# Expert tokens scattered chunk by chunk, tile results summed in DRAM by accumulating scatters, and a last norm that reads whole blocks

## The chip, the cores and the metric

The kernel runs on one core of one Trainium2 chip. The metric is the device time of one execution, in microseconds: the median of five runs of the kernel before is 2193.05 us (2187.0 to 2196.98). TensorE is called PE here, VectorE DVE, ScalarE ACT, GpSimd POOL and SyncE SP. PE, DVE, ACT and POOL each work through their own instructions strictly in order; a DMA is issued from SP's or POOL's instruction stream and then runs beside the engines.

## The reference

A decoder of two layers on 16 sequences of 128 tokens, 512 wide, all in float32. Every sub-layer ends in `x = layernorm(x + sublayer(x))`. The change lies in the last sub-layer, a mixture of experts:

```
logits = x @ gate_weight.T;  scores = softmax(logits)            # 2048 tokens, 8 experts
topk_w, topk_idx = top_k(scores, 2)
y  = sum over the 2 chosen experts e:  w_e * (silu(x @ g_e) * (x @ u_e)) @ down_e    # 352 wide
y += (silu(x @ sg) * (x @ su)) @ shared_down                     # shared expert, 704 wide
x  = layernorm(x + y)
```

## The kernel before

The activations lie on the chip throughout as 16 blocks `x[b]` of 128 tokens by 512. The five sub-layers before the experts are left as they are. During the cross attention ahead of the experts (`attend(p5, ...)`), SP issues, from `prepare(0)`, the shared expert's weights, one DMA that fills the DRAM buffer `slots_x` with zeros (L851; 39 tiles of 128 rows, 9,984 KB), and after it the context `ct` of group 2, which PE transposes at L864. SP's DMAs share one queue and start in the order of issue.

The expert stage has four parts.

Routing and the shared expert's hidden layer. DVE works out each token's two experts, their weights `w12`, and its two slots (`slots`), so that all tokens of one expert stand in whole tiles of 128 rows: the 32 blocks' worth of token copies and the padding make `NT` = 39 tiles. Beside it PE works on 24 chunks of the shared expert (`hidden(n, g)`, four groups `g` of 512 tokens, two halves `n` of three chunks each). A chunk is the matmuls `pg` and `pu` (L999), ACT's silu `sg` (L1006) and DVE's product `act` (L1007). PSUM has three banks for `pg` and two for `pu`, so PE can be about two chunks ahead of DVE.

Token scatter. Once the slots are known, POOL issues 32 indirect DMAs in a row (L1047): block `b` is written to its first slots and to its second slots in `slots_x`.

The loop over 39 tiles. A tile `t` has its expert's weights `ew`, 128 rows of 17,408 bytes gathered by one indirect DMA from POOL (L1060), in three buffers; and its tokens `xs`, read from `slots_x` by SP (L1065). The step of the loop is, on PE: transpose tile `step` (L1070), transpose the activations of tile `step-2` (L1092), gate and up of tile `step-1` (`rg`, `ru`, L1080), down of tile `step-2` (`ry`, L1101), and a share of the shared expert's down projection (`po`, L137). The weights of tile `s+3` can be asked for when the down matmuls of tile `s` have freed their buffer; gate and up of tile `s+3` come after the down matmuls of tile `s+1`. DVE copies `ry` to SBUF (L1105) and SP writes it to `slots_y` (L1106). `EARLY` = 7 blocks of the shared down projection (six matmul pairs each) are dealt over the 39 steps.

The end. For each block: one of the nine remaining shared down projections on PE, added to `x[b]` by DVE (L1113); two indirect reads of the block's rows from `slots_y`, issued by POOL (L1158); for each DVE's `x[b] += weight * y` (L1162); statistics on DVE (L110, L112, L114), the power for the reciprocal root on POOL (L116), a shift on DVE (L1146), the normalised block on ACT (L1147) and its write from SP (L1148). Two PSUM banks hold the shared down projection, so PE can be two blocks ahead of L1113.

The order within an engine is the scheduler's, within these dependences.

Of the kernel before, what the change touches and what calls it, by code (L numbers as in the profile page):

```python
# [45 lines left out]
def decoder_kernel(ctx: ExitStack, tc: tile.TileContext, a: dict, out: bass.AP):  # L46
# [40 lines left out]
        nc.sync.dma_start(t, src)  # L87
        return t

    x = [xp.tile([P, D], F32, tag=f"x{b}", name=f"x{b}") for b in range(NB)]  # L90

    def load_x(b0, b1):
        for b in range(b0, b1):
# [705 lines left out]
    def load_shared():  # L799
# [6 lines left out]
        for n in range(2):  # L806
# [13 lines left out]
            for copy in range(2):  # L820
                r = copy * h + n * last
                nc.sync.dma_start(sw_dn[r : r + last, 5, :], dn[h : h + last, 2])
    slots_x = dram.tile([NT * P, D], F32, tag="slots_x", name="slots_x")
    slots_y = dram.tile([NT * P, D], F32, tag="slots_y", name="slots_y")

    with tc.tile_pool(name="p5", bufs=1) as p5:
        gate = moe.tile([P, KC, 32], F32, tag="gate", name="gate")
# [2 lines left out]
        irev = load_const("irev", [P, E], a["irev"], moe)  # L830
        before = moe.tile([P, P], F32, tag="before", name="before")
        nc.vector.tensor_tensor(before, maskT, ident, ALU.subtract)
        count = moe.tile([P, NB + NT + 1], mybir.dt.int32, tag="count", name="count")
        nc.gpsimd.iota(count[:, 0:NB], [[P, NB]], base=0, channel_multiplier=0)
        nc.gpsimd.iota(count[:, NB : NB + NT], [[1, NT]], base=0, channel_multiplier=0)
        nc.gpsimd.iota(count[:, NB + NT :], [[1, 1]], base=0, channel_multiplier=1)
        ramp = moe.tile([P, NB + NT + 1], F32, tag="ramp", name="ramp")
        nc.vector.tensor_copy(ramp, count)
        wq5, wo5 = wqo5[:, 0], wqo5[:, 1]
        psum.share(mm=2, sc=4, pt=2)  # L840
# [2 lines left out]
        def prepare(g):  # L843
            if g == NG:
                return []
            ct = load_context(g) if g else ct0
            if g == 0:
                load_shared()
                zero = p5.tile([P, D], F32, tag="zero", name="zero")
                nc.gpsimd.memset(zero, 0.0)  # L850
                nc.sync.dma_start(  # L851
                    slots_x.rearrange("(n p) d -> p n d", p=P), zero.unsqueeze(1).broadcast_to([P, NT, D])
                )
            ctT = p5.tile([P, TG], F32, tag="ctT", name="ctT", bufs=2)
            xT = p5.tile([P, KC, TG], F32, tag="xT", name="xT", bufs=2)
            qT = p5.tile([P, KC, TG], F32, tag="qT", name="qT", bufs=2)
            kT = p5.tile([P, KC, TG], F32, tag="kT", name="kT", bufs=2)
            vs = [p5.tile([P, D], F32, tag="v", name="v", bufs=2 * GB) for _ in range(GB)]
            groups[g] = qT, kT, vs

            def turn_context():
                pk = bank("mm", [P, GB, P], "pk")
                for i in range(GB):
                    nc.tensor.transpose(pk[:, i, :], ct[:, i, :], ident)  # L864
                nc.scalar.copy(ctT, pk.rearrange("p b l -> p (b l)"))

            tasks = [(0.64, turn_context)]
            tasks += [(0.64, lambda i=i: transpose_x(xT, g * GB + i, i * P)) for i in range(GB)]
            for c in range(KC):
                cols = slice(c * P, (c + 1) * P)  # L870
                chain(
                    tasks, "pk2", [(wkv5[:, cols], ctT)], lambda pk2, c=c: nc.vector.tensor_copy(kT[:, c, :], pk2)
                )
                chain(
                    tasks, "pq", [(wq5[:, k, cols], xT[:, k, :]) for k in range(KC)],
                    lambda pq, c=c: nc.scalar.mul(qT[:, c, :], pq, 1.0 / math.sqrt(HD)),
                )
            for i in range(GB):
                chain(
                    tasks, "pv", [(ctT[:, i * P : (i + 1) * P], wkv5[:, D : 2 * D])],  # L880
                    lambda pv, i=i: nc.scalar.copy(vs[i], pv),
                )
            return tasks
# [28 lines left out]
    with tc.tile_pool(name="p6", bufs=1, reuse_waits="tile") as p6:  # L912
        acts, halves = {}, {}
        w12 = []
        slots = []
        which = p6.tile([P, NT], mybir.dt.int32, tag="which", name="which")

        def half_rows(g):
# [14 lines left out]
        with tc.tile_pool(name="p6a", bufs=1, side="right", reuse_waits="tile") as p6a:  # L933
# [48 lines left out]
            both = gt("both")  # L982
            nc.vector.tensor_tensor(both, chosen[0], chosen[1], ALU.add)

            def hidden(n, g):


                if n == 0:
# [3 lines left out]
                for m_ in range(3 * n, 3 * n + 3):  # L992
                    whole = m_ < 5
                    pg = bank("sc", [P, TG], "pg")
                    pu = bank("pt", [P, TG], "pu") if whole else pg[FS % P :]
                    for dst, off in ((pg, 0), (pu, P))[: 2 if whole else 1]:
                        at = 2 * m_ * P + off
                        for k in range(KC):
                            nc.tensor.matmul(  # L999
                                dst, lhsT=sw_gu[:, k, at : at + P], rhs=xTs[g][:, k, :],  # L1000
                                start=(k == 0), stop=(k == KC - 1),
                            )
                    sg = p6.tile([P, TG], F32, tag="sg", name="sg", bufs=3)
                    rows = slice(0, P) if whole else slice(0, FS % P)
                    act = acts[g][:, m_, :] if whole else halves[g // 2][half_rows(g)]
                    nc.scalar.activation(sg[rows], pg[rows], AF.Silu)  # L1006
                    nc.vector.tensor_tensor(act, sg[rows], pu, ALU.mult)  # L1007

            hidden(0, 0)


# [26 lines left out]
            for n in range(2):  # L1038
# [2 lines left out]
                sl = p6.tile([P, NB], mybir.dt.int32, tag=f"slot{n}", name=f"slot{n}")  # L1041
                nc.vector.tensor_copy(sl, m)
                slots.append(sl)
            views = dram_disjoint_views(slots_x, 2 * NB)
            for b in range(NB):
                for n in range(2):
                    nc.gpsimd.indirect_dma_start(  # L1047
                        out=views[2 * b + n], out_offset=bass.IndirectOffsetOnAxis(ap=slots[n][:, b : b + 1], axis=0),
                        in_=x[b], in_offset=None,
                    )  # L1050


        table = a["l1f_w"].rearrange("n p f -> (n p) f")
        with tc.tile_pool(name="p6r", bufs=1, side="right", reuse_waits="tile") as p6r:

            class Tile:
                def __init__(self, t):
                    self.t = t
                    self.w = p6.tile([P, EW], F32, tag="ew", name=f"ew{t}", bufs=3)
                    nc.gpsimd.indirect_dma_start(  # L1060
                        out=self.w, out_offset=None, in_=table,
                        in_offset=bass.IndirectOffsetOnAxis(ap=which[:, t : t + 1], axis=0),
                    )
                    self.x = p6r.tile([P, D], F32, tag="xs", name="xs", bufs=3)
                    nc.sync.dma_start(self.x, slots_x[t * P : (t + 1) * P, :])  # L1065

                def turn(self):
                    tr = bank("mm", [P, KC, P], "tr")
                    for k in range(KC):
                        nc.tensor.transpose(tr[:, k, :], self.x[:, k * P : (k + 1) * P], ident)  # L1070
                    self.xT = p6r.tile([P, KC, P], F32, tag="xsT", name="xsT", bufs=2)
                    nc.scalar.copy(self.xT, tr)  # L1072

# [23 lines left out]
                def down(self):  # L1097
                    dn = down_w(self.w)
                    po = bank("av", [P, D], "ry")
                    for m_, mw in enumerate(ECH):  # L1100
                        nc.tensor.matmul(  # L1101
                            po, lhsT=self.actT[:mw, m_, :], rhs=dn[:mw, m_, :], start=(m_ == 0), stop=(m_ == 2)
                        )
                    y = p6.tile([P, D], F32, tag="y", name="ry", bufs=6)
                    nc.vector.tensor_copy(y, po)  # L1105
                    nc.sync.dma_start(slots_y[self.t * P : (self.t + 1) * P, :], y)  # L1106

            def shared_down(tasks, b):
                g, i = divmod(b, GB)
# [3 lines left out]
                    lambda po: nc.vector.tensor_tensor(x[b], x[b], po, ALU.add),  # L1113
                )

            ahead = {0: Tile(0)}
            for g in range(NG):
                for n in range(2):
                    if (n, g) != (0, 0):
                        hidden(n, g)  # L1120
                if g % 2:
                    ahead[len(ahead)] = Tile(len(ahead))
            EARLY = 7
            tasks = []
            for b in range(EARLY):
                shared_down(tasks, b)
# [1 line left out]
            for step in range(NT + 2):  # L1128
# [7 lines left out]
                    ahead.pop(step - 2).down()  # L1136
                if 3 <= step + 2 < NT:
                    ahead[step + 2] = Tile(step + 2)
                if step < NT:
                    share.deal()  # L1140


            def normalize(b, stats):
                mean, rstd = stats
                shift = small.tile([P, 1], F32, tag="shift", name="shift")
                nc.vector.tensor_scalar(shift, mean, rstd, -1.0, ALU.mult, ALU.mult)  # L1146
                nc.scalar.activation(x[b], x[b], AF.Identity, bias=shift, scale=rstd)  # L1147
                nc.sync.dma_start(out[b], x[b])  # L1148

            norms = []  # L1150
            for b in range(NB):
                if EARLY + b < NB:
                    tasks = []
                    shared_down(tasks, EARLY + b)
                    Share(tasks, 1).deal()
                for n in range(2):
                    y = p6.tile([P, D], F32, tag="y", name="yb", bufs=6)
                    nc.gpsimd.indirect_dma_start(  # L1158
                        out=y, out_offset=None, in_=slots_y,
                        in_offset=bass.IndirectOffsetOnAxis(ap=slots[n][:, b : b + 1], axis=0),  # L1160
                    )
                    nc.vector.scalar_tensor_tensor(x[b], y, w12[n][:, b : b + 1], x[b], ALU.mult, ALU.add)  # L1162
                norms.append((b, statistics(b, nc.vector)))
                if b:
                    normalize(*norms.pop(0))
            normalize(*norms.pop(0))
    psum.close()


# [122 lines left out]
```

## Time and profile before

| | |
|---|---|
| median of five runs | 2193.05 us (2187.0 to 2196.98) |
| the profiled execution | 2198.35 us, its span 2196.5 us |
| PE busy over the span | 2093.7 us, 95% |
| DVE, ACT, POOL busy | 880.8, 632.7, 502.1 us |
| 32 token scatters on POOL, L1047 | 31.1 us, 972 ns each |
| 39 weight gathers on POOL, L1060 | 36.9 us, 945 ns each |
| 32 reads of `slots_y` on POOL, L1158 | 32.3 us, 1009 ns each |
| software DMA queue (all indirect DMAs) | 103.68 MB, 12.8% of 16 engines over the span |
| from the last `ry` matmul's end to the span's end | 74.7 us (2121.8 to 2196.5) |

The span is the time from the first to the last profiled instruction of the program; the execution's time is 1.85 us longer. Busy time is summed over the span; a busy PE says which engine is full but not at which place an end is set, so the stages are read one by one. A wait "A <- B: us, times, longest" says how long A's engine stood still before A until B was done. "remote" stands where the profile cannot name what released it.

### The profile page before, as it was taken

How to read it: one execution, taken by the hardware profiler on the slowest of the kernel's cores; microseconds unless marked ns; L12 is line 12 of the kernel's file. 1: busy time of each engine (PE TensorE's matmuls, PEld its weight loads, DVE VectorE, ACT ScalarE, POOL GpSimd, SP SyncE). 2: the span in 40 equal slices, each digit the busy share in tenths (PEclk: the TensorE clock that was granted, in tenths of full speed). 3: DMA queues.
4: the chain of work that ended last, by engine and by line, in shares of the span. 5: the costliest groups of instructions: out<-in, count | busy, mean ns of one | idle time of the engine just before them, and what ended most of it. 6: DMA issues, size and time to landing. Idle time of an engine off the chain costs nothing.

```text
span 2196.5 us, 26727 instructions
## 1 busy us (share of the span) xinstructions
PE 2093.7 (95%) x10265; PEld 1178.2 (54%) x10265; DVE 880.8 (40%) x1700; ACT 632.7 (29%) x2174; POOL 502.1 (23%) x590
## 2 busy tenths in 40 slices
PE   7999997999999999999999999999898999999995
PEld 4555553445445458888555544555443455555542
DVE  4667644544333244222123324777430122122236
ACT  3555421333333222222211114566410111111102
POOL 4443320212111112323211101333232001001125
PEclk9999998999999999999999999999999999999998
DMA  5000253211000010001200026000033077787745
GB/s 220 1 33 33 102 149 99 70 38 33 6 10 6 1 40 14 1 1 50 99 1 1 1 56 223 1 1 1 1 118 131 2 266 298 292 299 296 290 173 177
DMA packets 73776, 199.63 MB, mean 91 GB/s; under 512 B 19760, under 2 KB 35504, under 8 KB 66992
## 3 DMA queue, kind: packets, MB, share of 16 engines
q1 hardware_dynamic: 62912, 94.24, 13.2%
q0 software_dynamic: 10736, 103.68, 12.8%
q8 instruction: 81, 1.33, 0.2%
q14 instruction: 47, 0.39, 0.1%
HBM read 163.82 MB, written 34.08 MB: 90 GB/s over the span
## 4 chain that ended last, share of the span: by engine, by line
PE 68%; issue 16%; DVE 6%; POOL 4%; DMA 3%; ACT 1%; another core or an unknown queue 1%; SPq 0%; POOLq 0%; ACTq 0%; DVEq 0%
PE po L572 10%; PE po L148 7%; PE pq L742 5%; PE pq L137 5%; PE pq L518 4%; PE pa L654 4%; PE pb L654 4%; PE po L681 4%; PE pg L999 3%; PE pu L999 3%; PE av L559 3%; PE pv L750 3%; DMA piece<-in_l0f_w_dram 2%; PE pt L203 2%; PE sc L535 2%
## 5 line engine op out<-in xcount | busy, mean ns | idle before, releaser
L198 POOL TENSOR_TENSOR p<-p,rs 128x512 f32<-128x512 f32 x192 | 199.3, 1039 | 579.3 <-DVE rs L197 567.1
L572 PE MATMUL po<-mT,cc 128*128 128x512 f32 x512 | 237.5, 608 | 0.0
L191 ACT ACTIVATE p<-t,nmx 128x128 f32<-128x128 f32 x512 | 198.6, 390 | 53.3 <-DVE nmx L186 27.4
L572 PEld LDWEIGHTS po<-mT,cc 128*128 128x128 f32 x512 | 92.9, 191 | 108.1 <-issue 104.4
L1060 POOL DMA_INDIRECT ew<-in_l1f_w_dram,which x39 | 36.9, 945 | 441.0 <-PE ry L1101 310.0
L191 ACT ACTIVATE p<-sc,nmx 128x128 f32<-128x128 f32 x256 | 90.0, 373 | 141.7 <-DVE nmx L186 131.4
L518 PE MATMUL pq<-xT,wqr 128*128 128x512 f32 x256 | 119.2, 609 | 0.9 <-ACT xT L128 0.7
L148 PE MATMUL po<-wo,oT 128*128 128x512 f32 x256 | 117.8, 604 | 1.0 <-ACT mT L292 0.6
L742 PE MATMUL pq<-xT,wq 128*128 128x512 f32 x256 | 110.9, 594 | 1.0 <-ACT xT L128 0.7
L1080 PE MATMUL rg<-ew,xsT 128*128 128x352 f32 x312 | 100.9, 466 | 6.3 <-DMA ew<-in_l1f_w_dram,which 6.2
L1101 PE MATMUL ry<-ew,ractT 128*128 128x512 f32 (+1 forms) x234 | 106.9, 592 | 0.0
L114 POOL TENSOR_SCALAR ve<-mv 128x1 f32<-128x1 f32 x80 | 17.9, 223 | 371.9 <-DVE mv L112 356.8
L1080 PE MATMUL ru<-ew,xsT 128*128 128x352 f32 x312 | 98.7, 459 | 0.0
L191 ACT ACTIVATION_READ_ACCUMULATOR p<-t,nmx 128x1 f32 x512 | 96.4, 188 | 0.0
L203 PEld LDWEIGHTS pt<-ident,p 128*128 128x128 f32 x512 | 60.5, 143 | 62.8 <-issue 50.8
L1087 DVE TENSOR_TENSOR ract<-rsg,ru 128x352 f32<-128x352 f32 x39 | 20.3, 521 | 175.1 <-issue 165.6
L203 PE MATMUL pt<-ident,p 128*128 128x128 f32 x512 | 79.4, 279 | 11.3 <-DVE pT L205 7.1
L121 DVE TENSOR_SCALAR x<-x,mv,rstd 128x512 f32<-128x512 f32 x80 | 53.7, 672 | 88.3 <-POOL rstd L116 88.3
L205 DVE COPY pT<-pt 128x512 f32<-128x512 f32 x128 | 86.7, 680 | 5.6 <-PE pt L203 5.3
L999 PE MATMUL pg<-xT,sw_gu 128*128 128x512 f32 x192 | 86.5, 593 | 0.0
L1072 ACT COPY xsT<-tr 128x512 f32<-128x512 f32 x39 | 22.8, 585 | 218.6 <-PE tr L1070 201.1
L137 PE MATMUL po<-sw_dn,act 128*128 128x512 f32 x160 | 78.3, 609 | 6.6 <-DVE ve L114 3.0
(210 smaller groups left out, 3676.4 us busy)
## 6 DMA issues: line engine op xcount, KB each, us to landing
piece<-in_l0f_w_dram SPq DMA_DIRECT2D x48, 352.0 KB, 3.3
raw<-in_l0x_raw_dram SPq DMA_DIRECT2D x8, 1728.0 KB, 6.9
slots_x<-zero SPq DMA_DIRECT2D x1, 9984.0 KB
xs<-slots_x SPq DMA_DIRECT2D x39, 256.0 KB, 9.0
slots_y<-ry SPq DMA_DIRECT2D x39, 256.0 KB, 2.2
x<-in_x_dram SPq DMA_DIRECT2D x16, 256.0 KB, 6.5
rep<-dkv SPq DMA_DIRECT2D x64, 64.0 KB, 1.9
out_dram<-x SPq DMA_DIRECT2D x16, 256.0 KB, 3.0
```

Of the source, the lines that this page charges most:

```text
L137: nc.tensor.matmul(got["p"], lhsT=lhsT, rhs=rhs, start=(n == 0), stop=(n == len(pairs) - 1))
L148: nc.tensor.matmul(po, lhsT=oT[:, c, :], rhs=wo[:, c, :], start=(c == 0), stop=(c == KC - 1))
L191: nc.scalar.activation(self.p[:, j, :], src[:, j, :], AF.Exp, bias=nmx[:, j : j + 1], accum_out=self.sm[:, j : j + 1])
L198: nc.gpsimd.tensor_tensor(self.p, self.p, spread(rs, P), ALU.mult)
L203: nc.tensor.transpose(pt[:, j, :], self.p[:, j, :], ident)
L518: nc.tensor.matmul(pq, lhsT=wqr[:, k, cols], rhs=xT[:, k, :], start=(k == 0), stop=(k == KC - 1))
L572: nc.tensor.matmul(self.po, lhsT=self.cc[:, 4 * par + j, :], rhs=mT[h], start=(par == 0 and j == 0), stop=(par == 1 and j == 3),)
L654: nc.tensor.matmul(dst, lhsT=wt[:, k, f * P : (f + 1) * P], rhs=xs[n][:, k, :], start=(k == 0 and n == 0), stop=(k == KC - 1 and n == 1),)
L742: nc.tensor.matmul(pq, lhsT=wq4[k // 2][:, k % 2, c * P : (c + 1) * P], rhs=xT[:, k, :], start=(k == 0), stop=(k == KC - 1))
L999: nc.tensor.matmul(dst, lhsT=sw_gu[:, k, at : at + P], rhs=xTs[g][:, k, :], start=(k == 0), stop=(k == KC - 1),)
L1080: nc.tensor.matmul(dst, lhsT=self.xT[:, k, :], rhs=gu[:, k, off : off + FE], start=(k == 0), stop=(k == KC - 1),)
L1101: nc.tensor.matmul(po, lhsT=self.actT[:mw, m_, :], rhs=dn[:mw, m_, :], start=(m_ == 0), stop=(m_ == 2))
```

## The change

There are four changes, all in the expert stage.

1. The blocks get four more columns (`xw`, 516 wide; `x[b]` is columns 2 to 513). In front and behind stand a token's weight and its token number, for the second and the first expert. `slots_x` rows are 516 wide. After the first three chunks, each chunk's end (`send`) lets POOL wait for the chunk's `act` (a copy of one column, `beat`) and then issue the two scatters of one block. The first weights are asked for after the third block's scatters.
2. A tile reads its rows' weight and token number with its tokens. `ry` is multiplied by the weight as it leaves PSUM, and POOL issues an indirect DMA that adds the tile's rows to the tokens' rows of a new DRAM buffer `sums` (padding rows go to rows past the tokens). `slots_y` and SP's writes to it are gone. `sums`, 55 blocks of 128 rows by 512, is zeroed by a second DMA right after that of `slots_x`. Since an addition reads and writes its rows, each of these scatters waits for the one before it to have landed.
3. At the end, SP reads `sums` in 16 plain blocks; POOL adds each to `x[b]`; the 32 indirect reads and DVE's 32 multiply-adds are gone. Epsilon, power and shift are made for two blocks at a time.
4. `EARLY` is 8, and the eight blocks left are dealt over seven parts of the end.

```diff
-    x = [xp.tile([P, D], F32, tag=f"x{b}", name=f"x{b}") for b in range(NB)]
+    xw = [xp.tile([P, D + 4], F32, tag=f"x{b}", name=f"x{b}") for b in range(NB)]
+    x = [t[:, 2 : D + 2] for t in xw]
...
-    slots_y = dram.tile([NT * P, D], F32, tag="slots_y", name="slots_y")
+    slots_x = dram.tile([NT * P, D + 4], F32, tag="slots_x", name="slots_x")
+    sums = dram.tile([(NB + NT) * P, D], F32, tag="sums", name="sums")
...
+                for t, rows, width in ((slots_x, NT, D + 4), (sums, NB + NT, D)):
+                    nc.sync.dma_start(
+                        t.rearrange("(n p) d -> p n d", p=P), zero[:, 0:width].unsqueeze(1).broadcast_to([P, rows, width])
+                    )
...
+                    if then is not None:
+                        then(act)
...
             for b in range(NB):
                 for n in range(2):
-                    nc.gpsimd.indirect_dma_start(
-                        out=views[2 * b + n], out_offset=bass.IndirectOffsetOnAxis(ap=slots[n][:, b : b + 1], axis=0),
-                        in_=x[b], in_offset=None,
-                    )
+                    at = D + 2 - n * (D + 2)
+                    nc.vector.tensor_copy(xw[b][:, at : at + 2], infos[n][:, b, :])
+        def send(act):
+            if unsent:
+                b = unsent.pop(0)
+                tc.keep_in_program_order(nc.gpsimd.tensor_copy(beat[0 : act.shape[0]], act[:, 0:1]))
+                for n in range(2):
+                    at = 2 - 2 * n
+                    tc.keep_in_program_order(nc.gpsimd.indirect_dma_start(
+                        out=views[2 * b + n], element_offset=at,
+                        out_offset=bass.IndirectOffsetOnAxis(ap=slots[n][:, b : b + 1], axis=0),
+                        in_=xw[b][:, at : at + D + 2], in_offset=None,
+                    ))
...
+                    info = p6r.tile([P, 2], F32, tag="tell", name="tell", bufs=6)
+                    nc.vector.tensor_tensor(info, self.x[:, 0:2], self.x[:, D + 2 : D + 4], ALU.add)
+                    self.weight = info[:, 0:1]
+                    self.place = p6r.tile([P, 1], mybir.dt.int32, tag="place", name="place", bufs=6)
+                    own = NC + NB + self.t
+                    nc.vector.tensor_tensor(self.place, info[:, 1:2], ramp[:, own : own + 1], ALU.add)
...
-                    nc.vector.tensor_copy(y, po)
-                    nc.sync.dma_start(slots_y[self.t * P : (self.t + 1) * P, :], y)
+                    nc.vector.tensor_scalar(y, po, self.weight, None, ALU.mult)
+                    nc.gpsimd.indirect_dma_start(
+                        out=sums, out_offset=bass.IndirectOffsetOnAxis(ap=self.place, axis=0),
+                        in_=y, in_offset=None, compute_op=ALU.add,
+                    )
...
-            EARLY = 7
+            EARLY = 8
...
+            share = Share(tasks, NB // 2 - 1)
+            for b in range(NB):
+                if b % 8 == 0:
+                    y = p6.tile([P, 8, D], F32, tag="ew", name=f"sum{b}", bufs=3)
+                nc.sync.dma_start(y[:, b % 8], sums[b * P : (b + 1) * P, :])
+                ys.append(y[:, b % 8])
...
+            for b in range(0, NB, 2):
+                if share.part < share.parts:
+                    share.deal()
+                mv = small.tile([P, 2, 2], F32, tag="mv2", name="mv2")
+                for i in range(2):
+                    nc.gpsimd.tensor_tensor(x[b + i], x[b + i], ys[b + i], ALU.add)
+                    st = small.tile([P, 6], F32, tag="st", name="st")
+                    nc.vector.bn_stats(st, x[b + i])
+                    nc.vector.bn_aggr(mv[:, i], st)
+                normalize(b, mv)
```

## The prediction

> **What bounds the kernel now.** PE is 95% busy, so the questions are where the other 5% lies in the stages that change, and what each edit puts in its place. I read the stages' windows first, then the waits, then the timeline at the two places where PE stands still.
>
> The windows (per engine: busy us and instructions; then granted clock, DMA share, GB/s):
>
> ```profile
> core 0: us, PE busy (x) PEld busy (x) DVE busy (x) ACT busy (x) POOL busy (x), PEclk, DMA share, GB/s
> ...
> 1650.00:1672.00 22.00, 15.99 (x37) 6.82 (x36) 1.34 (x2) 1.68 (x3) 12.27 (x13) 0.89 0.52 201
> 1672.00:1755.00 83.00, 83.00 (x193) 36.67 (x192) 8.96 (x13) 7.15 (x12) 0.98 (x1) 0.99 0.07 27
> ...
> 1790.00:2080.00 290.00, 284.45 (x964) 163.26 (x963) 60.20 (x129) 32.50 (x62) 28.28 (x31) 1.00 0.79 294
> ...
> 2122.00:2197.00 75.00, 49.77 (x104) 18.53 (x102) 43.17 (x106) 13.01 (x16) 42.12 (x48) 0.88 0.57 172
> ```
>
> Three places: a hole of 6 us in the chunks while the scatters run; the tile loop, where PE is full (284.45 of 290) and the DMA engines nearly so (0.79); and the end, 75 us of which PE works 50. The waits:
>
> ```profile
> POOL ew L1060 <- PE ry L1101: 310.0, 36, 14.0
> ...
> ACT sg L1006 <- remote: 24.7, 2, 12.8
> DVE act L1007 <- remote: 21.6, 1, 21.6
> ...
> PE rg L1080 <- DMA ew<-in_l1f_w_dram,which: 6.2, 12, 1.4
> PE pu L999 <- DVE act L1007: 6.0, 1, 6.0
> ```
>
> During the 32 scatters (1625.3 to 1665.9) ACT and DVE stood up to 21.6 us before `sg` and `act`, though PE's matmuls for them were done, until 1670.2, when the scatters had landed; PE filled its PSUM banks and then stood 6.0 us. In the loop POOL is idle until PE's down matmuls free a buffer, and PE meets late weights in 12 steps: PE and the weights' latency are level.
>
> The timeline of the end (start, duration; in brackets the idle before):
>
> ```profile
> 2119.03 2.74 PE L1101 MATMUL ry<-ew,ractT 128*128 128x512 f32 x6
> ...
> 2164.57 6.25 PE L137 MATMUL po<-sw_dn,act 128*128 128x512 f32 x10 [3.03 <-DVE ve L114]
> ...
> 2177.22 1.12 PE L137 MATMUL po<-sw_dn,half 64*128 64x512 f32 x2
> ...
> 2187.52 0.81 ACT L1147 ACTIVATE x<-x,shift,rstd 128x512 f32<-128x512 f32 x1 [3.43 <-DVE shift L1146]
> ```
>
> From the last `ry` (2121.8) PE needs 56.5 us to its last matmul (2178.3), then 10.0 us pass to ACT's last end (2188.3) and 8.2 to the span's end. A block's down projection takes 5.54 us (2125.33 to 2130.87 from one block's start to the next), and 1.7 us of the nine (a row of four matmuls at 2117.31) lie ahead of that `ry`: 9 x 5.54 - 1.7 = 48.2. So PE lost 8.3 us to DVE's queue and to the slower matmuls after a stall (ten in 6.25 us instead of 4.56).
>
> **The change, part by part.** The sum is made against the profiled execution, 2198.35 us, which is 5.3 us above the median.
>
> *Scatters in pairs.* Two scatters per chunk of 6.87 us instead of 32 in 41 us. POOL is otherwise idle there; the last pair goes after the 19th chunk, five chunks (34 us) ahead of the loop. PE waits for nothing on POOL. The cause of the late releases is not named in the profile; they began after about 18 scatters had followed one another, and nothing of the kind stands elsewhere. I take it that they go: 6.0 us of standing, and 1.8 us since the eight matmuls after it took 5.23 us instead of 3.43. Gain 7.8 (between 0, if they come anyway, and 7.8). DVE's 32 copies of two columns (147 ns like L114) and four small pieces, about 5.5 us, follow the slots at 1625.6 and end at 1631.2, 0.5 us past the next `act` (1630.7): PE, two chunks ahead, covers that. The weights of tile 0 are asked for some 25 us later, and are first needed at 1756.8.
>
> *A second zero fill.* The first fills 4992 rows from 1331 to about 1358 at 352 GB/s, DMA share 0.98. 7040 rows more take 27 x 7040/4992 = 38 us, to 1396, and the context of group 2 is behind them in SP's queue: it lands at about 1400. PE transposes it at 1404.3 and all behind it on PE would wait. Margin 4 us; rows of 2,064 bytes could use it up. I take 1 us (0 to 8, if the first fill's rows run 25% slower and cost 7 us, and the rest 5).
>
> *The loop: DVE and SP.* The weighted copy is read from PSUM as the copy was (692 ns); two small DVE pieces per tile, 0.3 us, lie in DVE's idle time (60 of 290 us busy). SP loses 39 writes. Nothing on the path.
>
> *The loop: the adding scatters.* POOL issues one per step (about 1 us) and has 9.4 us (tile 3's weights are issued at 1770.88, tile 38's at 2099.64: 9.39 a step). Order on POOL: weights of `s+3`, adding scatter of `s`, weights of `s+4`. The scatter is queued behind 2.2 MB of weights, whose last rows end 10.1 us after their issue, so it lands some 13 us after it, and the next scatter waits for that: about 4 us into the next step. That wait holds up the following weights only if it grows by 4 us more.
> What counts is the DMA engines' time. By the packet records a weight row takes 648 ns, eight rows on each engine 5.2 us; next to it 0.67 for `xs` (8 x 84 ns) and 0.67 for the write of `y`, which goes. A plain scatter of 256 KB takes 4 packets of 159 ns on each engine, 0.64 us. No row shows an addition. Its floor is that plain price; its ceiling is eight rows one after another at the latency of a first packet after a pause (1.0 to 1.8 us, mostly 1.2), 9.6 us. Packets in this queue follow each other without such gaps (648 ns on end), so I take it near the floor: one more row moved per row written, 1.3 us. Between the weights' last rows (10.1) and the next weights' first (9.4 + 2.2) the queue has 1.5 us free. So most of it is hidden; I let a quarter of the added 0.6 us delay the weights. The price of 1 us of delay: weights of `s+3` land, gate and up 4.74, down 2.57, and two steps have passed, so half a microsecond a step, 18 us over 36 steps. 0.17 x 18 = 3 us.
> The Trainium skill (Collectives: The Full Stack, "Why ReduceScatter is half of AllGather") has it that an addition in the DMA path costs no adder time but a second source read on the same ring, so that the rate halves. By it the scatter takes twice the plain 0.64 us and the 3 us stand; by the plain row alone the ring gains nothing and loses nothing and the 3 us fall away. No run here shows an addition yet.
>
> *One block more in the loop.* 12 matmuls, 5.2 us at the `po` pace of 0.86 a pair. Where PE waits for weights (12 of 36 steps) they cost nothing: 4 (3 to 5.2).
>
> *The end.* Before the first sum can be read, the scatters of tiles 36 to 38 must land one after another: `ry` 0.9, issue 1.0, landing 2 to 3, then SP's read, about 8 us after the last `ry`; the first `slots_y` read came after 9.1 (2130.92). From there POOL needs 16 adds at 1.27 us (L729, the same shape) and 8 powers at 0.57: 25 us, done 33 us after the last `ry`. PE needs 8 x 5.54 - 1.7 = 42.6. In DVE's order the sum of the third block left stands behind the statistics of block 9, which POOL reaches about 21 us after the last `ry`; PE wants that bank at 22. So PE stands little: 1 us (0 to 8.3, its loss now). Behind PE's last matmul: DVE's add 0.7, POOL's 1.3, statistics 0.9, epsilon 0.15, power 0.55, shift 0.2, two blocks on ACT 1.6, hand-overs 0.5: 5.9 us instead of 10.0, since no indirect read's multiply-adds are left. The end: 42.6 + 1 + 5.9 + 8.2 = 57.7 instead of 74.7, gain 17.0.
>
> *Sum:* 2198.35 - 7.8 + 1 + 3 + 4 - 17.0 = 2181.6; by the median, 5.3 less, 2176.
>
> **The rivals.**
> *The addition is slow* (slower). The one mechanism: an adding scatter holds its queue for x us an engine, and the next weights wait. Over the 1.5 us that are free each microsecond costs 18. For: the DMA share of 0.79, PE already meeting late weights, and that each row must be read before it can be written. Against: POOL's and the queue's free gap. The other terms gain 19.8, so it decides from x = 2.6, four plain scatters. At x = 4: 45 us instead of 3, 2218. At the ceiling of 9.6 a step has 5.2 + 0.7 + 9.6 = 15.5 instead of 9.4: +220, about 2393.
> *The late releases stay.* If scatters as such, not their density, hold up ACT and DVE, 7.8 us stay: 2184. For: the cause is not named. Against: the waits begin only after 18 of them.
> *The end does not shrink.* If POOL's adds, DVE's order or the serial scatters hold PE's two banks as the reads do now, its 8.3 us of loss stay, and a late context takes its 8: 2176 + 7 + 7 = 2190.
>
> **How the numbers follow.** Five runs spread by 0.45%; I count under 0.3%, 6.6 us, as no change: 2186.5 to 2199.6. My forecast 0.54 (2166 to 2186, from no loop cost and no stall at all to 10 us of them); late releases 0.10, most of it still faster; the end as it is 0.09; slow addition 0.27, nearly all past 2199.6. Faster 0.61, same 0.12, slower 0.27. The range runs from 2166 to 2225, where a slow addition of x = 4 is inside and only its far part is out.
>
> **What would show it.** Right: no "remote" wait in the chunks and PE's windows full there; no wait of PE for `ct` near 1404; a step of 9.3 to 9.5 us with PE's waits for `ew` under 10 us; about 58 us from the last `ry` to the span's end, PE without holes in it. Wrong: steps of 10 us and more with PE waiting for `ew`, scatters landing over 13 us after their issue, POOL standing before weights on an earlier scatter; or the second fill in the way of `ct`.

## The result, and the profile after

The changed kernel took 2201.18 us (median of 33 runs, 2196.16 to 2207.95), the kernel before 2195.74 us (59 runs). The ratio is 1.0032, with a 95% interval of 1.0023 to 1.0040: a third of a per cent slower, where 0.8% faster was forecast. The profiled execution took 2201.42 us (span 2199.6). The same windows of it (busy us and instructions per engine; then granted clock, DMA share, GB/s):

```profile
core 0: us, PE busy (x) PEld busy (x) DVE busy (x) ACT busy (x) POOL busy (x), PEclk, DMA share, GB/s
...
1360.00:1404.00 44.00, 42.90 (x286) 23.87 (x284) 33.20 (x65) 31.82 (x136) 15.68 (x17) 1.00 0.98 357
...
1650.00:1672.00 22.00, 22.00 (x53) 9.80 (x52) 2.07 (x3) 1.79 (x3) 7.33 (x10) 1.00 0.19 72
...
1790.00:2080.00 290.00, 273.50 (x922) 154.95 (x921) 60.42 (x185) 30.46 (x59) 75.01 (x59) 1.00 0.84 276
...
2122.00:2200.00 78.00, 62.17 (x142) 25.44 (x140) 28.60 (x66) 12.51 (x17) 27.32 (x27) 0.92 0.42 130
```

The hole among the chunks is closed: 22.00 of 22 us, where it was 15.99. The second fill fills the DMA engines (0.98) and PE doesn't mind. But the loop, where PE was busy for 284.45 of 290 us, now has 273.50. Its waits, from 1755 to 2139 us (engine, line, waited for: us in total, times, longest us):

```profile
engine line waited for: us in total, times, longest us
DVE tell L1108 <- DMA xs<-slots_x: 263.1, 34, 9.0
POOL ew L1093 <- PE ry L1143: 223.2, 36, 20.1
...
PEld rt L1134 <- DVE ract L1129: 26.2, 23, 4.8
PE rt L1134 <- DVE ract L1129: 20.8, 21, 4.5
```

PE no longer waits for weights (it was 6.2 us in 12 steps). It waits for `ract`, a DVE instruction that it never met late before. And DVE, idle for most of the loop, has a wait that didn't exist: `tell`, on the token load `xs`. One step in the timeline shows how the two belong together (first PE, then DVE: start, duration, in brackets the idle time before and what ended it):

```profile
1953.85 2.53 PE L1122 MATMUL ru<-ew,xsT 128*128 128x352 f32 x8
...
1959.65 0.60 PE L1106 MATMUL tr<-ident,xs 128*128 128x128 f32 x4
1961.68 0.55 PE L1134 MATMUL rt<-ident,ract 128*128 128x128 f32 x3 [1.43 <-DVE ract L1129]
```

```profile
1961.00 0.16 DVE L1108 TENSOR_TENSOR tell<-xs 128x2 f32<-128x2 f32 x1 [8.70 <-DMA xs<-slots_x]
1961.11 0.52 DVE L1129 TENSOR_TENSOR ract<-rsg,ru 128x352 f32<-128x352 f32 x1
```

PE had finished `ru` of tile 20 at 1956.38, so `ract` could have run then. It ran at 1961.11, since `tell` stood ahead of it in DVE's queue. That `tell` belongs to tile 24: its load was issued at 1951.19, its last row ended 9.2 us later, and PE turns tile 24 only at 1979.18. The scheduler had put DVE's reading of the tile right behind the tile's load, four tiles ahead, in front of work that PE needed at once.

By stages, worked out from the starts and ends of PE's instructions in the traces (us; the forecast is the sum of its steps; the fifth column is an experiment below):

| stage | before | forecast | after | `tell` held |
|---|---|---|---|---|
| to the first routing matmul `plT` | 1583.7 | 1584.7 | 1584.8 | 1576.9 |
| chunks, to the first `rg` | 173.1 | 165.3 | 165.3 | 165.3 |
| loop, first `rg` to last `ry` | 365.0 | 372.0 | 388.9 | 363.6 |
| last `ry` to PE's last matmul | 56.6 | 43.6 | 50.2 | 51.3 |
| PE's last to the span's end | 18.2 | 14.1 | 10.4 | 10.4 |

The first row is the same code but for the fill, and lies between 1576 and 1585 in all the profiles of this case; the long ones have the lower granted clock there (0.98 at 1584.8 us here, 0.99 at 1576.2 in the last experiment). The other rows repeat within 2 us where the code is the same. So the forecast failed in the loop, by 17 us, and at the end by 3.

### The profile page after: what moved, and what is told of

It reads as the page before. It is cut to its first block, busy times and chain, and to the rows that moved or that the text cites. A ratio compares the mean times of both kernels' runs of the same rounds, so it can differ in the third digit from the quotient of the medians.

```text
span 2199.6 us, 26823 instructions
## 1 busy us (share of the span) xinstructions
PE 2095.7 (95%) x10265; PEld 1180.1 (54%) x10265; DVE 868.0 (39%) x1766; ACT 631.9 (29%) x2174; POOL 544.6 (25%) x624
## 4 chain that ended last, share of the span: by engine, by line
PE 78%; DMA 9%; DVE 6%; issue 3%; POOL 2%; ACT 1%; ACTq 0%; SPq 0%; POOLq 0%; DVEq 0%
PE po L574 10%; PE po L150 7%; DMA xs<-slots_x 6%; PE pq L744 5%; PE pq L139 5%; PE pq L520 4%; PE pg L1008 4%; PE pa L656 4%; PE pb L656 4%; PE po L683 4%; PE pu L1008 3%; PE ry L1143 3%; PE av L561 3%; PE rg L1122 3%; PE pv L752 2%
## 5 line engine op out<-in xcount | busy, mean ns | idle before, releaser
L1108 DVE TENSOR_TENSOR tell<-xs 128x2 f32<-128x2 f32 x39 | 6.3, 161 | 272.9 <-DMA xs<-slots_x 272.9
L205 PEld LDWEIGHTS pt<-ident,p 128*128 128x128 f32 x512 | 60.2, 142 | 62.2 <-issue 53.3
L1114 ACT COPY xsT<-tr 128x512 f32<-128x512 f32 x39 | 22.8, 585 | 226.6 <-PE tr L1106 197.4
L667 POOL TENSOR_TENSOR hl<-ht,hh 128x512 fp32r<-128x512 f32 x44 | 58.1, 1320 | 116.7 <-ACT hh L665 116.7
```

What stands on the lines that cost most here:

```text
L205: nc.tensor.transpose(pt[:, j, :], self.p[:, j, :], ident)
```

## The experiments

All of them stand against runs of the kernel before on the same chip.

**`tell` held in its place.** One line of the changed kernel:

```diff
-                    nc.vector.tensor_tensor(info, self.x[:, 0:2], self.x[:, D + 2 : D + 4], ALU.add)
+                    tc.keep_in_program_order(
+                        nc.vector.tensor_tensor(info, self.x[:, 0:2], self.x[:, D + 2 : D + 4], ALU.add)
+                    )
```

> The changed kernel with one thing altered: `tell`, the small DVE addition that reads a fetched tile's side columns, is held in DVE's order where the program writes it (behind the weighted copy `ry` of the step before) instead of where the scheduler put it (ahead of `ract`, some 21 us before PE turns the same tile). Theory A, DVE's queue: in the changed kernel's loop DVE stood 263 us in 34 waits for the token loads `xs`, with `ract` queued behind, and PE lost 20.8 us in 21 waits for `ract`, 4.5 of it at the loop's start. If that is the cause, the waits of DVE for `xs` go, PE's waits for `ract` go, PE meets late weights again as before (6 us), the step falls from 9.88 to 9.4-9.5 us, first `rg` to last `ry` falls from 388.9 to 369-373 us, and the time to 2181-2185 us. Theory B, the transfers: if the adding scatters take so much of the DMA engines that loads land late, the wait only moves to the weights or to `xs` on PE; the step stays at 9.8-9.9 and the time at 2198-2204 us.

Measured: 2170.0 us, ratio 0.9877 (0.9852 to 0.9903). In the loop PE waited for one thing only (the same columns as the waits above):

```profile
PE rg L1124 <- DMA ew<-in_l1f_w_dram,which: 2.5, 2, 1.5
```

And DVE in one step (the columns of the timeline):

```profile
1922.32 0.52 DVE L1131 TENSOR_TENSOR ract<-rsg,ru 128x352 f32<-128x352 f32 x1 [4.58 <-PE ru L1124]
...
1924.83 0.75 DVE L1149 TENSOR_SCALAR ry<-ry,tell 128x512 f32<-128x512 f32 x1 [1.99 <-PE ry L1145]
...
1925.50 0.15 DVE L1109 TENSOR_TENSOR tell<-xs 128x2 f32<-128x2 f32 x1
```

`ract` now waits for PE, not for a load, and `tell` waits for nothing: its tile has long landed. The loop fell from 388.9 to 363.6 us, below the kernel before, though it holds a block more. The time fell further than I had expected (2181 to 2185), because I had put back the late weights of the kernel before (6 us), of which 2.5 came, and the 3 us of the forecast for the addition, of which the loop shows next to nothing (below). By their ratios the two changed kernels lie 34 us apart, by the stages behind the first routing matmul 24; the rest shows in none of these stages and stays open.

**The one instruction alone, in the kernel before.**

```diff
                         nc.tensor.transpose(tr[:, k, :], self.x[:, k * P : (k + 1) * P], ident)
+                    info = p6r.tile([P, 2], F32, tag="tell", name="tell", bufs=6)
+                    nc.vector.tensor_tensor(info, self.x[:, 0:2], self.x[:, D - 2 : D], ALU.add)
```

> The kernel before with one instruction added per tile: DVE adds two columns of the fetched tile `xs` to two others (128 x 2) into a small tile that nobody reads. Everything else, the scatters in one block, plain writes, the indirect reads at the end, stays as before; here too the scheduler has put the small addition ahead of `ract`. Theory A: this one instruction of 0.16 us brings most of the loop's loss: DVE waits for `xs` in some 35 steps, PE for `ract` in 20 or more, the step rises from 9.39 to 9.7-9.9 us and the time by 10 to 20 us, to 2206-2216. Theory B: 39 x 0.16 us beside idle time of DVE: 2194-2198 us.

Measured: 2215.47 us, ratio 1.0087 (1.0063 to 1.0110); the step 9.71 us, the loop 381.9 instead of 365.0. Its waits, with the same columns as above:

```profile
DVE tell L1072 <- DMA xs<-slots_x: 263.9, 35, 9.1
...
PE rt L1094 <- DVE ract L1089: 20.8, 22, 3.7
```

An addition of 128 x 2 elements that nobody reads costs 17 us of loop, with no adding scatter in the kernel. Its 39 executions are busy for 6 us.

**Plain scatters for adding ones, twice.** First in the changed kernel as it is:

```diff
-                        in_=y, in_offset=None, compute_op=ALU.add,
+                        in_=y, in_offset=None,
```

> The changed kernel with plain scatters in place of the adding ones (same rows, same queue, same waits); it leaves out the addition of a token's two results, so the sums hold only one of them. Theory A, DVE's queue: nothing of what `ract` waits for has changed; PE still loses about 20 us to it: 2196-2203 us. Theory B, the addition's own transfers: the step falls to 9.4-9.5 us and the time to 2181-2186 us. By my forecast's own term the addition is worth 3 us at most, if its cost shows in the loop at all.

Measured: 2199.63 us, ratio 1.0023 (1.0006 to 1.0040). The loop took 389.8 us, against 388.9 with the addition: the addition is not what lengthened it. Then the same edit with `tell` held:

> The kernel with `tell` held in place, and plain scatters in place of the adding ones; it leaves out the addition of a token's two results. This is the price of the addition where DVE's queue no longer hides it. An adding scatter's rows took 8 x 184 ns on each engine, plain ones 4 x 160 ns: 0.83 us a step less. With `tell` held PE has 2.5 us of waits for weights left. If the addition's time lies in the queue's gaps: 2168-2171 us, the same as with it. If it delays the weights by the quarter that I took: up to 2.5 us less, 2167-2168 us. The slow addition of my rival (45 us and more) would show as a far larger gain, which the 2.5 us that are left to wait for rule out.

Measured: 2168.23 us, ratio 0.9858 (0.9837 to 0.9879); the loop 362.9 against 363.6 and, in a second profile of the kernel with `tell` held, 363.0. The addition costs the loop at most 0.7 us (362.6 to 363.6 us with it in four profiles, 362.9 without), too little to tell from nothing. Its transfers do take longer, 184 ns on average for each of eight rows on an engine against 160 ns for a pair of rows: 1.47 against 0.64 us, and POOL is busy for 1.59 instead of 0.99 us.

What the addition costs lies at the end. DVE, POOL and ACT work through the same instructions in the same order there, with additions and with plain writes, but with plain writes PE needs 43.8 us from the last `ry` to its last matmul, where the two profiles with additions have 51.3 and 49.8 (without `tell` held 43.7 against 50.2). The last tile's scatter waits until the one before it has landed. As an addition it was issued 2.8 to 3.3 us after the last `ry` and its last row ended 4.3 to 4.4 us later; as a plain write, 1.1 and 2.4. So POOL's first additions of the read sums begin 10.3 to 10.8 us after the last `ry`, and 6.6 to 6.7 with plain writes (POOL in the changed kernel, whose last `ry` ends at 2139.0; then POOL and PE in this one, 2109.7):

```profile
2149.26 4.42 POOL L1222 TENSOR_TENSOR x<-x,sum 128x512 f32<-128x512 f32 x4 [6.00 <-DMA sum<-sums]
```

```profile
2116.36 4.23 POOL L1224 TENSOR_TENSOR x<-x,sum 128x512 f32<-128x512 f32 x4 [4.68 <-DMA sum<-sums]
...
2131.22 4.56 PE L139 MATMUL po<-sw_dn,act 128*128 128x512 f32 x10 [1.31 <-DVE x L1160]
```

PE's longest stop in the end is 1.31 us here and 4.35 with additions. Behind PE's last matmul 3.4 us of the gain are lost again (13.8 instead of 10.4; see the last section).

**The scatter issued twice, into one table and into two.** Both with `tell` held.

```diff
                         in_=y, in_offset=None, compute_op=ALU.add,
                     )
+                    nc.gpsimd.indirect_dma_start(
+                        out=sums, out_offset=bass.IndirectOffsetOnAxis(ap=self.place, axis=0),
+                        in_=y, in_offset=None, compute_op=ALU.add,
+                    )
```

> The kernel with `tell` held in place, and each adding scatter issued twice; the sums hold each result twice. It asks from where the rival of the slow addition decides. A second scatter adds 8 x 184 ns = 1.47 us to every engine's step (5.2 for weights, 0.67 for `xs`, 1.47 for the first: 8.8 of 9.33 us) and 1.6 us to POOL's. By my forecast's rule (1.5 us free, each further us costs 18) 2.94 us of scatter cost 26 us: about 2196 us. If the free time is larger than I took: 2170-2180. If POOL stands until the first scatter has landed (some 8 us) before it may issue the second, and the next weights are queued behind that: the step grows by several us, 2230 us and more.

Measured: 2376.99 us, ratio 1.0816 (1.0796 to 1.0836), a step of 14.94 us. My rule gave 2196; the last of the three cases came, and stronger. POOL and PE in the timeline, one step:

```profile
1997.74 4.05 PE L1124 MATMUL rg<-ew,xsT 128*128 128x352 f32 x8 [3.49 <-DMA ew<-in_l1f_w_dram,which]
...
1999.68 1.55 POOL L1154 DMA_INDIRECT sums<-ry,place  x1 [8.35 <-DMA sums<-ry,place]
...
2001.54 1.00 POOL L1093 DMA_INDIRECT ew<-in_l1f_w_dram,which  x1 [0.31 <-issue]
```

The second scatter waits 8.35 us for the first to land, and the next weights are queued behind it on POOL. To tell that wait from the transfers, the second scatter then went to a table of its own (`out=spare`, the same size):

> The kernel with `tell` held in place; behind each adding scatter a second one adds the same rows to a second table of the same size that nobody reads (nor fills first). The same DMA work and the same 1.6 us of POOL as with each scatter issued twice into one table (2377 us, step 14.94), but the second no longer waits for the first to land. If the engines' and POOL's time made the 206 us: about 2377 again. If it was the wait (POOL stood 294 us in 39 waits for the first scatter, with the next weights queued behind): by my forecast's rule of 18 us per us over the free 1.5 us, 2.94 us of scatters cost 26 us, 2190-2205; with more room in the queue than I took, 2170-2185.

Measured: 2181.14 us, ratio 0.9935 (0.9915 to 0.9954). The loop took 371.8 us, 8 to 9 more than with one scatter, and PE met late weights again (8.8 us in 9 waits). So 2.94 us of adding transfers a step cost 8 us, not the 26 of my rule, and nearly all of the 207 us was the wait with what followed from it. With both scatters in one table the loop grew by 195 us (558.2): 117 are standing, and most of the rest are matmuls behind a stop, at a lower granted clock (0.88 over the loop, 1.00 with one scatter); the eight of `rg` above took 4.05 us instead of 2.53. These scatters are dear on POOL by what they wait for, not by what they move.

**The scatters spread, in the kernel before.** The token scatters two per chunk, the tiles fetched after them; nothing else of the change:

```diff
+        def send(act):
+            if unsent:
+                b = unsent.pop(0)
+                tc.keep_in_program_order(nc.gpsimd.tensor_copy(beat[0 : act.shape[0]], act[:, 0:1]))
+                for n in range(2):
+                    tc.keep_in_program_order(nc.gpsimd.indirect_dma_start(
...
-                        hidden(n, g)
-                if g % 2:
+                        hidden(n, g, send)
+                if g != 2:
```

> The kernel before with its 32 token scatters issued two per chunk, after each chunk's activations, instead of one after another; the tiles are fetched after the last of them; the rest as before. My forecast gave this part a gain of 7.8 us: no wait of ACT or DVE that ends on a late release, PE's 22 us window from 1650 full, 2188 us (2186-2190). Its rival, that the late releases come with scatters as such: 2195-2197 us and the same waits of 10 to 20 us elsewhere in the chunks.

Measured: 2188.55 us, ratio 0.9969 (0.9955 to 0.9983). The chunks took 165.3 us from the first routing matmul to the first `rg`, as in the changed kernel, instead of 173.1. Then the same kernel with all 32 scatters behind the first chunk:

```diff
             if unsent:
-                b = unsent.pop(0)
                 tc.keep_in_program_order(nc.gpsimd.tensor_copy(beat[0 : act.shape[0]], act[:, 0:1]))
+            while unsent:
+                b = unsent.pop(0)
                 for n in range(2):
```

> The kernel before with everything that the spread version of it has (weights of tile 0 asked for later, tiles fetched after the scatters, POOL's small copy that ties the first scatter to a chunk), but all 32 scatters behind the first chunk, one after another. If the density of the scatters makes ACT and DVE see PE's releases late: waits of 10 to 20 us of ACT `sg` and DVE `act` that end with the last scatters' landing, 6 to 8 us of PE's time lost, 2194-2198 us. If one of the other alterations brought the 7 us of the spread version: no such waits, 2187-2190 us.

Measured: 2200.62 us, ratio 1.0024 (1.0010 to 1.0037), the chunks 175.4 us, and the late releases are back:

```profile
ACT sg L1006 <- remote: 26.4, 2, 25.5
DVE act L1007 <- remote: 19.0, 1, 19.0
```

So it is the scatters' following one another that delays the releases of PE; what in the chip does it stays open.

**The block more in the loop.** With `tell` held, `EARLY = 7` instead of 8.

> The kernel with `tell` held in place, and seven blocks of the shared down projection in the loop, as before, so nine after it. The block's 12 matmuls take 5.2 us in the loop, less what lies in waits for weights (6 us in the kernel before; 2.5 with eight blocks), and 5.5 us at the end. If PE's time is what the loop takes: the same, 2169-2172 us. If the loop had room for the block (it went into waits for weights), leaving it for the end costs up to 4 us: 2172-2175 us.

Measured: 2168.54 us, ratio 0.9853 (0.9829 to 0.9878), the same as with eight. Seven blocks leave 356.6 us of matmuls and 4.4 us of standing in the loop, eight leave 360.8 and 2.7: the block brings 4.2 us of work and takes 1.7 us of standing away.

**The end.** In the changed kernel PE's losses are these (the same columns of the timeline):

```profile
2163.60 0.66 DVE L1158 TENSOR_TENSOR x<-x,po 128x512 f32<-128x512 f32 x1
...
2164.31 7.21 PE L139 MATMUL po<-sw_dn,act 128*128 128x512 f32 x10 [4.35 <-DVE x L1158]
...
2188.08 1.12 PE L139 MATMUL po<-sw_dn,half 64*128 64x512 f32 x2
...
2193.35 1.52 ACT L1210 ACTIVATE x<-x,shift,rstd 128x512 f32<-128x512 f32 x2 [9.57 <-DVE shift L1208]
```

PE stands 0.69 and 4.35 us for a sum `x<-x,po` that stands behind statistics in DVE's queue, and these wait for POOL's additions. It takes 7.21 instead of 4.56 us for the ten matmuls after the longer stop, at a granted clock of 0.63; after the shorter one it was 1.00 and they took 4.56. With `tell` held it is the same (5.8 us of standing). So the statistics were held behind the sums as well, and the eight blocks left dealt over eight parts of the end instead of seven; the two were not run apart:

```diff
-            share = Share(tasks, NB // 2 - 1)
+            share = Share(tasks, NB // 2)
...
-                    nc.vector.bn_stats(st, x[b + i])
+                    tc.keep_in_program_order(nc.vector.bn_stats(st, x[b + i]))
```

> The kernel with `tell` held in place (2170.0 us), and the end's statistics `st` held in DVE's order behind the sums `x<-x,po` written before them, one block dealt to each of the eight pairs. Theory: at the end too DVE's order is what PE lost by. PE stood 5.8 us in two waits for `x<-x,po`, whose DVE instruction stood behind statistics that waited for POOL, and ran ten matmuls in 7.2 instead of 4.56 us after the longer wait: 8 us together, the part that my forecast of the end (PE 42.6 us and 1 us of standing after the last `ry`, measured 51.2) lacked. If so, last `ry` to PE's last falls from 51.2 to 43-45 us and the time to 2162-2164 us. Rival: POOL's 16 additions are what the end waits for, and PE's standing is only their reflection; then the statistics end no earlier, ACT's last stays, and the time is 2168-2172 us.

Measured: 2166.47 us, ratio 0.9850 (0.9829 to 0.9871). From the last `ry` PE needs 43.9 us (forecast 43.6) instead of 51.3. PE's one wait there:

```profile
PE po L139 <- DVE x L1160: 1.4, 1, 1.4
```

This is the fastest by its ratio, 1.5% under the kernel before, though 0.9853 with seven blocks lies inside its interval. That the end's 7 us are in the time, too, the ratios can't say: those with and without them overlap. I ran the kernel with only `tell` held again, beside one that has the end's alteration and the last four blocks' additions on DVE instead of POOL:

> The kernel with only `tell` held in place once more, on the same chip as the next one, so that the two can be compared: 0.985 to 0.990 of the kernel before.

> The kernel with `tell` held in place and the end's statistics behind the sums `x<-x,po` (eight pairs), and the last four blocks' additions of the read sums on DVE instead of POOL. The end from the last `ry` was 61.7 us with `tell` held alone and 54.4 with the statistics held; DVE adds in 0.69 us where POOL took 1.09, without a hand-over to POOL and back: 1 us more at the very end. If my reading of the end holds: 8 us less than with `tell` alone, about 0.982 of the kernel before. If the end is hidden otherwise: no less than with `tell` alone.

Measured: 2169.04 us and 0.9862 (0.9838 to 0.9887) with `tell` alone; 2165.23 us and 0.9861 (0.9842 to 0.9880) with both. The ratios show no difference, the medians 4 us. In the profiles the end took 60.2 and 56.0 us from the last `ry`; it was 54.4 with the additions left on POOL. PE needed 46.1 us instead of 43.9, but not through DVE's additions: its one stop, 2.03 us instead of 1.43, with 6.09 us for the ten matmuls after it, ends at 2120.86, and the first of those additions ran at 2134.8. Behind PE's last matmul they brought 0.4 us (10.0 instead of 10.4), where I had expected 1. My expectation of 0.982 failed.

## Why the forecast was wrong, step by step

*Scatters in pairs: -7.8.* Right: the chunks fell by 7.8 us, and the spread alone brings 7 us. The rival that the late releases stay is out, and the guess that density makes them is shown by the dense version.

*A second zero fill: +1.* Nothing to see. In the 70 us from 1330 PE is busy for 68.09 us with one fill and with two, at DMA shares of 0.43 and 0.97. That the first stage met the forecast (1584.7 and 1584.8) is luck, since it varies by 9 us.

*The loop, DVE and SP: 0.* This is the step that failed. "Two small DVE pieces per tile, 0.3 us, lie in DVE's idle time" counted what they occupy (0.16 us each) and not what they wait for. `tell` reads `xs`, which in the kernel before only PE read; so DVE got a wait for a load of 9.3 us, and behind that wait stood `ract`, for which PE waits. It cost about 25 us: the loop is 388.9 us with it and 363.6 without. Of the 23.9 us by which the loop grew over the kernel before, 16.5 are more standing (22.8 instead of 6.3) and 7.5 more matmul time, 4.2 of that the block and the rest mostly the last transpose ahead of each stop, which counts in full there (0.27 us), where otherwise the next matmul follows after 0.11. The trace of before couldn't show this wait, but the order of the changed kernel's instructions on DVE did: `tell` with its wait on a load, one place ahead of `ract`. The forecast drew on this order for POOL, and for DVE at the end, but not for DVE in the loop.

The Trainium skill (PSUM — Partial Sum Buffer, "Engine vs sequencer instructions") says that "ScalarE/VectorE/GpSimdE queues are strict FIFO". The trace agrees: `ract` ran 4.7 us after its operands were there, 0.11 us after `tell` began. By that sentence alone the step should have been asked of DVE's queue, as I asked it of POOL's.

*The adding scatters: +3.* Too high in the loop: 0.7 us at most. The size of the transfer was nearly right (1.3 taken, 1.47 measured), POOL's issue was not (1 taken, 1.59 measured), and the last row ended 8.0 to 8.4 us after the issue (median), not 13. The price of 18 us for each us over 1.5 was too high as well: at 2.94 us of transfers 26 were due and 8 came. The rule that I weighed there (the Trainium skill, Collectives: The Full Stack, "Why ReduceScatter is half of AllGather": an addition needs a second source read, which halves the rate) comes near the size: twice the plain price by the rule, 2.3 times measured. It says nothing of the 0.6 us more on POOL. The rival of the slow addition was wrong as I put it, by transfers. It would have decided through a wait, had there been two scatters a step.

*One block more: +4.* The loop's matmul time grows by 4.2 us and 1.7 us of standing go; over the profiles with eight blocks 1.6 to 2.6 us remain.

*The end: 57.7 us, measured 60.6.* Two terms were mis-sized, with opposite signs. PE's standing and the slower matmuls after it were put at 1 us and measured 7.6. The forecast had the right place, the sum behind the statistics of block 9 in DVE's order, but the wrong times: POOL was to begin 8 us after the last `ry` and to reach block 9 at about 21, with 2 to 3 us for a scatter to land. In the trace the last two scatters landed 5.3 and 4.4 us after their issue, POOL began at 10.3 and was done with block 9 at 23.4, and PE wanted the bank at 21.0. So POOL's late start and DVE's order made the loss together: plain writes take it away with the order unchanged, and the changed order with POOL's start unchanged. And the 8.2 us from ACT's last end to the span's end were taken as fixed and measured 4.8. The 5.9 us in between were 5.7.

So with `tell` held, the sum of the forecast (2176) is nearly what is measured (2170.0), in part by luck: in the loop the addition and the block cost 4 to 5 us less, and some 4 us more are missing that no run explains (with seven blocks and the additions 361.0 us, 365.0 before); the end takes 7 us more, the close 3.4 less. And the changed kernel's 2201 us lies where the forecast had put its rival of a slow addition, but not for that rival's reason.

## What to carry over

A new instruction costs what it waits for, not what it occupies: for each one that reads a transfer's result, look up where the scheduler has put it on its engine and what stands behind it. An engine that is idle for four fifths of a stage still holds up another, when the little that it does comes in the wrong order. The same question is worth asking of a DMA issue on an engine's queue: a second scatter that waits for the first cost 207 us here, one that doesn't 12.

## What was not expected of the hardware

After the last instruction the span ends with POOL's closing drain, not with the last output's landing: in the kernel before the drain takes 9.09 us and ends 7.4 us after ACT's last, while SP's own, behind the last output, ends after 2.4. With adding scatters the drain is shorter: 9.81 us with 39 plain ones in their place (both kernels), 6.46 with 39 adding ones, 2.94 with 78. So with plain scatters the span ends 3.4 us later after PE's last matmul than with adding ones (13.8 instead of 10.4). What the drain waits for, no run here shows.

Behind the longer stops of the end PE came back at a lower clock. Behind stops of 0.69, 1.31 and 1.43 us the granted clock was 1.00 and the ten matmuls of a block took 4.56 us. Behind 2.03 us it was 0.74 and they took 6.09, behind 4.35 us 0.63 and 7.21. At which length it begins, and why, no run here shows.
